# Cross attention of a decoder layer: the sums of the exponentials of groups 0 and 2 go from TensorE to VectorE, and four smaller steps change place

## The chip, the cores and the metric

One core of one Trainium2 chip runs the whole kernel. The metric is the device time of one execution in microseconds (us); lower is better. Engines are named as the profile names them: PE is TensorE (matmuls; PEld its weight loads), DVE is VectorE, ACT is ScalarE, POOL is GpSimd, SP issues most DMAs.

## The reference

Four batch entries of 512 rows and 512 columns, float32, 16 heads of 32 columns. The output is x after three steps:

```python
x = x + attn(layernorm(x), q_w, q_b, k_w, k_b, v_w, v_b, o_w, o_b)  # causal, masked to -inf
x = x + xattn(layernorm(x), ctx, ctx)   # heads of layernorm(x) as queries, of ctx as keys and values
x = x + ffn(layernorm(x), W_up, W_down, W_gate, W_expert)

# xattn, per head:
scores = einsum('bhqd,bhkd->bhqk', qh, kh) / sqrt(hd)
scores = where(causal, scores, -10000.0)          # a finite bias: masked keys keep a weight
out    = einsum('bhqk,bhkd->bhqd', softmax(scores), vh)
# ffn: relu(x Wup) Wdown + (sum of the softmax of the two largest gate logits) * (x Wexpert)
```

Because the masked bias of cross attention is finite, the kernel adds what the masked keys weigh: the weight of one masked key (`count`, from the row's maximum) times the sum of the values behind the diagonal (`beh_t`), and times their number (`cnt`) in the denominator.

## The kernel before

Everything is kept in float32 (the maxima's rows in bf16). The order on PE, DVE, ACT and POOL is the order in which the program issues its instructions (`tc.manual_schedule`); each engine works through its own queue, and a buffer of a pool is handed out again once its last reader is done. PSUM is four buffers of two banks (`pair`): scores, values' products, projections and transposes all take turns in them. In SBUF, `act` has one buffer per tag, `work` two unless `bufs` says otherwise.

The main loop runs over the batch entries b = 0 to 3. For each:

- `with_maxima` (L826) for self attention: ten units of score matmuls (L286), whose row maxima are needed for the softmax. ACT copies the scores (L297), POOL masks the diagonal (L305), DVE takes maxima (L317) and splits them into bf16 parts (`split`, L334 to L343). Between the units PE does filler: projections of the same or the next entry and the feed-forward part (`ffn`) of the entry before. `rows(g)` (L345) lets PE transpose the parts of one group of four heads into a row (L349), which DVE or ACT copies out (L355).
- `attend` (L869): ten units u0 to u9 of scores with the maximum subtracted (`scores`, L383 and L394), exponentials on ACT (L414), masks on POOL (L422). Two units later `values` (L434, matmuls on L453) multiplies them with v. In the units, (g, j) is head group g and block j of 128 keys: (0,0); (0,3),(0,1); (0,2),(1,2); (1,0); (1,3),(1,1); then the same for groups 2 and 3.
- the denominators. In `shares`, u = 0 is the product with v and u = 1 the product with `ones`, that is the sum of the exponentials. For groups in `self.added` the sums are made on DVE instead: `add_up` (L478) adds each block's exponentials into the block-0 tile (`self.sums`), and one set of four matmuls (`summed`, L487) reduces it over the keys. In self attention that holds for groups 0 to 2, in cross attention for none. `inverse` (L506) transposes, inverts and transposes back on DVE; `scale` (L502) multiplies on POOL; `divide` (L518) does the whole of it for the other groups, in cross attention with the masked keys' part added (L523, L524) before, and the product (L528) on DVE.
- `out_projection` (L657): the product with wo (`pm_o`, L663), transposes of ctx as filler, then the layer norm for the queries of cross attention (L675, L194 to L206).
- the same again for cross attention, and `add_cross` (L686): PE transposes the result (`tp_x`, L691), DVE adds it to x and takes the layer norm for `ffn`.

What only cross attention has: `behind(e, c)` (L643), a running sum from the right of the context's columns on DVE (L648), issued in `attend` before each group's first block; and `masked(g)` (L359): one matmul that spreads the row's maximum (L362), one exponential on ACT (L364), and two multiplications on DVE (L367 for the values, L368 for the count), issued in `attend` after units 2, 4, 7 and 9.

The feed-forward part of entry b runs as filler later: for b = 1 its expert matmuls lie in the maxima stage of self attention of b = 3 (`expert`, weighed into x by DVE on L790), for b = 2 its up and down projections lie in the maxima stage of cross attention of b = 3 (`down`, added to x by DVE on L775).

Of the kernel before, what the change touches and what calls it, by code (L numbers as in the profile page):

```python
# [9 lines left out]
F32 = mybir.dt.float32  # L10
# [16 lines left out]
def decoder_layer(  # L27
# [234 lines left out]
    class Attention:  # L262
        def __init__(self, q_t, k_t, v, cross, name):
            self.q_t, self.k_t, self.v, self.cross, self.name = q_t, k_t, v, cross, name
            self.nm, self.mrow, self.pv, self.out = {}, {}, {}, None
            self.more, self.sums, self.rden, self.e = {}, {}, {}, None
            self.added = () if cross else range(NC - 1)

        def maxima(self, pieces):

# [87 lines left out]

        def masked(self, g):  # L359

            bc = pair(f"mb_{self.name}_{g}")
            nc.tensor.matmul(bc[:, 0, :], lhsT=same, rhs=self.mrow[g], start=True, stop=True)  # L362
            count = work.tile([P, S], F32, tag="count", name=f"ct_{self.name}_{g}")
            nc.scalar.activation(count, bc[:, 0, :], AF.Exp, bias=mbias)  # L364

            beh = self.e.beh_t[:, g, :]
            nc.vector.scalar_tensor_tensor(beh, count, 1.0, beh, ALU.min, ALU.mult)  # L367
            nc.vector.scalar_tensor_tensor(count, count, 1.0, cnt, ALU.min, ALU.mult)  # L368
            self.more[g] = (beh, count)

        def scores(self, pieces):


            at, N = [], 0
            for g, j in pieces:
                at.append(N)
                N += S - j * P
            name = f"{self.name}_{pieces[0][0]}_{pieces[0][1]}"
            scs = [pair(f"sc_{name}_{n}") for n in range(2)]
            for (g, j), c in zip(pieces, at):  # L380
                for r in range(HG):
                    h = slice(r * HD, (r + 1) * HD)
                    nc.tensor.matmul(  # L383
                        scs[r // 2][:, r % 2, c : c + S - j * P],
                        lhsT=self.k_t[h, g, j * P : (j + 1) * P],
                        rhs=self.q_t[h, g, j * P :],
                        start=(c == 0),
                        stop=False,
                        skip_group_check=(len(pieces) > 1),
                    )  # L390
            for (g, j), c in zip(pieces, at):
                for r in range(HG):
                    h = slice(r * HD, (r + 1) * HD)
                    nc.tensor.matmul(  # L394
                        scs[r // 2][:, r % 2, c : c + S - j * P],
                        lhsT=onesb[h, :],
                        rhs=self.mrow[g][h, j * P :],
                        start=False,
                        stop=True,
                        skip_group_check=(len(pieces) > 1),  # L400
                    )
            g, j = pieces[0]
            pts = []
            if j == 0 and g in self.added:

                self.sums[g] = act.tile(
                    [P, 2, 2, S], F32, tag=("ck_t", "beh_t")[g % 2], name=f"sum_{name}"
                )
            for n in range(2):
                if j == 0 and g in self.added:  # L410
                    pt = self.sums[g][:, n]
                else:
                    pt = work.tile([P, 2, S], F32, tag="pt", name=f"pt_{name}_{n}", bufs=6)
                nc.scalar.activation(pt, scs[n], AF.Exp)  # L414

                if len(pieces) == 1:
                    diagonal = pt[:, :, :P].unsqueeze(2)
                elif j == pieces[1][1]:
                    diagonal = pt.rearrange("p u (k q) -> p u k q", k=2)[:, :, :, :P]
                else:  # L420
                    diagonal = pt[:, :, : 2 * P].rearrange("p u (k q) -> p u k q", k=2)
                nc.gpsimd.affine_select(  # L422
                    out=diagonal,
                    in_=diagonal,
                    compare_op=ALU.is_ge,
                    fill=0.0,
                    base=0,
                    pattern=[[0, 2], [0, len(pieces)], [1, P]],
                    channel_multiplier=-1,
                )  # L430
                pts.append(pt)
            return [(g, j, c, pts) for (g, j), c in zip(pieces, at)]
# [8 lines left out]
        def shares(self, g, blocks):  # L441

            js = {j for j, *_ in blocks}
            first = js == {0} if g % 2 == 0 else js == {2}
            last = js == {2} if g % 2 == 0 else 1 in js
            if first:
                self.pv[g] = pair(f"pv_{self.name}_{g}")
            pv = self.pv[g]
            for u in range(1 if g in self.added else 2):
                for n, (j, c, pts) in enumerate(blocks):  # L450
                    for r in range(HG):
                        h = g * HG + r
                        nc.tensor.matmul(  # L453
                            pv[r * HD : (r + 1) * HD, u, j * P :],
                            lhsT=ones if u else self.v[:, j, h * HD : (h + 1) * HD],
                            rhs=pts[r // 2][:, r % 2, c : c + S - j * P],
                            start=first,
                            stop=last and n == len(blocks) - 1,
                            skip_group_check=True,
                        )  # L460
            if first and g == 0 and not self.cross:
                self.out = act.tile([P, NC, S], F32, tag="o_t", name=f"oT_{self.name}")
            if (first if g in self.added else js == {0}) and g - 1 in self.added:
                self.sum_in = pv if g in self.added else pair(f"ls_{self.name}")
                self.summed(g - 1, self.sum_in)
            if js == {0} and g - 2 in self.added:
                self.scale(g - 2)
            if 1 in js and g - 1 in self.added and g not in self.added:
                self.spread(g - 1, self.sum_in)
                self.scale(g - 1)  # L470
            if last and g in self.added:
                nc.scalar.copy(self.out[:, g, :], pv[:, 0, :])
                if g > 0:
                    self.spread(g - 1, pv)
            elif last:
                self.divide(g)

        def add_up(self, made):  # L478
            for g, j, c, pts in made:
# [21 lines left out]

        def scale(self, g):  # L502
            o = self.out[:, g, :]
            nc.gpsimd.tensor_tensor(o, o, self.rden.pop(g), ALU.mult)

        def inverse(self, g, den):  # L506
            name = f"{self.name}_{g}"
# [8 lines left out]
            return den_t  # L516

        def divide(self, g):  # L518
            pv = self.pv.pop(g)
            num, den = pv[:, 0, :], pv[:, 1, :]  # L520
            if self.cross:
                beh, count = self.more.pop(g)
                nc.vector.tensor_tensor(count, den, count, ALU.add)  # L523
                nc.vector.tensor_tensor(beh, num, beh, ALU.add)  # L524
                num, den = beh, count
                self.out = self.e.beh_t
            rden = self.inverse(g, den)
            nc.vector.tensor_tensor(self.out[:, g, :], num, rden, ALU.mult)  # L528


    class Entry:
# [125 lines left out]
    def out_projection(e, a, sides):  # L657
# [3 lines left out]
        for c in range(NC):  # L661
# [7 lines left out]
                )  # L669
            if c < NC - 1:  # L670
                run(sides[c::3])

        def add(t):
            xi = e.x[:, t, :]
# [38 lines left out]
    def ffn(e):  # L713
# [55 lines left out]
        def down(t):  # L769
            if t % 2 == 0:  # L770
                made["d"] = pair(f"pm_d{b}_{t}")
            yield from project(made["d"][:, t % 2, :], made["h"], wdown_sb, t)
            if t % 2 == 1:
                both = e.x[:, t - 1 : t + 1, :]
                nc.vector.tensor_tensor(both, made["d"], both, ALU.add)  # L775

        def expert(t):
# [5 lines left out]
                made["e"] = pair(f"pm_e{b}_{t}")  # L783
            yield from project(made["e"][:, t % 2, :], f_t, wexp_sb, t)
            for n in (0,) if last else (0, 1) if t % 2 == 1 else ():
                weigh(t - t % 2 + n, made["e"][:, n, :], slice(0, D), nc.sync)

        def weigh(t, ps, cols, queue):
            xt = e.x[:, t, cols]
# [36 lines left out]
    def with_maxima(steps, a, first=0, norms=()):  # L826
# [16 lines left out]
        for n, pieces in enumerate(units):  # L843
# [6 lines left out]
            for k in range(count):  # L850
                next(fill, None)
                done += 1
                if k == min(1, count - 1) and n in (5, 7):
                    jobs = a.rows((n - 5) // 2) + jobs
                if n == len(units) - 1 and k == count - (2 if count > 4 else 1):
                    if total >= 2 * len(units):
                        a.rows(2)[0](nc.scalar.copy)
# [11 lines left out]
    def attend(a, late):  # L869
# [3 lines left out]
        for g in range(0, NC, 2):  # L873
            units += [[(g, 0)], [(g, 3), (g, 1)], [(g, 2), (g + 1, 2)]]
            units += [[(g + 1, 0)], [(g + 1, 3), (g + 1, 1)]]
        waiting, held = [], []

        def values():
            made = waiting.pop(0)
# [9 lines left out]
        for n, pieces in enumerate(units):  # L889
# [3 lines left out]
                    copy(nc.scalar.copy)  # L893
            if len(waiting) > 2:
                values()
            if a.cross and pieces[0][1] == 0:
                behind(a.e, pieces[0][0])
            if a.cross and n % 5 in (2, 4):
                a.masked(pieces[0][0])
        while waiting:  # L900
            values()

    with tc.manual_schedule(engines=BY_HAND):
# [11 lines left out]
        for b in range(B):  # L915
# [15 lines left out]
            run(steps[2:3])  # L931
            norm_cross(e, made, 2)
            ca = Attention(e.cq_t, e.ck_t, e.cv, True, f"c{b}")
            ca.e = e
            late = with_maxima(steps[3:], ca)
            if b + 2 < B:
                after.x = load_x(b + 1)
# [77 lines left out]
```

## Time and profile before

| | |
|---|---|
| median of 3 runs | 817.24 us (816.1 to 817.62) |
| the profiled execution | 814.9 us, span of its instructions 813.2 us |
| granted TensorE clock | 1.0 |
| PE busy | 802.2 us (99%) |
| DVE busy | 538.4 us (66%) |
| ACT busy | 395.6 us (49%) |
| POOL busy | 288.7 us (36%) |
| `pv_c` with `ones` (L453) | 512 matmuls, 43.2 us |
| `pv_c` with cv (L453) | 512 matmuls, 44.1 us |
| scans `behT` (L648) | 16, 20.5 us on DVE |
| additions `sum_s` (L483) | 72, 59.8 us on DVE |

The busy time of PE counts matmuls that overlap in the pipeline, so what a matmul costs is better read from the starts of the one and of the next in the timeline. A line of a timeline has the start, the time from the first to the last instruction of a run of equal ones, engine, source line, operation, result and operands, sizes, how many, and in brackets how long the engine was idle before and what ended that. Times are in us from the start of the span.

### The profile page before, as it was taken

How to read it: one execution, taken by the hardware profiler on the slowest of the kernel's cores; microseconds unless marked ns; L12 is line 12 of the kernel's file. 1: busy time of each engine (PE TensorE's matmuls, PEld its weight loads, DVE VectorE, ACT ScalarE, POOL GpSimd, SP SyncE). 2: the span in 40 equal slices, each digit the busy share in tenths (PEclk: the TensorE clock that was granted, in tenths of full speed). 3: DMA queues.
4: the chain of work that ended last, by engine and by line, in shares of the span. 5: the costliest groups of instructions: out<-in, count | busy, mean ns of one | idle time of the engine just before them, and what ended most of it. 6: DMA issues, size and time to landing. Idle time of an engine off the chain costs nothing.

```text
span 813.2 us, 14284 instructions
## 1 busy us (share of the span) xinstructions
PE 802.2 (99%) x5808; PEld 383.4 (47%) x5808; DVE 538.4 (66%) x930; ACT 395.6 (49%) x446; POOL 288.7 (36%) x485
## 2 busy tenths in 40 slices
PE   8999999999999999999999999999998999999998
PEld 7444554444444454444544445444444444444544
DVE  2478835868678834586867773687779844997512
ACT  2457426861546514566145752686166714574110
POOL 4334612342234732234233481244233643333100
PEclk9999999999999999999999999999999999999999
DMA  9600000001010000030100000000100100000101
GB/s 337 232 27 28 1 1 1 1 2 53 1 27 27 2 1 1 0 106 2 52 14 14 1 2 0 1 1 2 53 26 27 53 1 0 1 2 2 52 0 52
DMA packets 13681, 24.52 MB, mean 30 GB/s; under 512 B 1968, under 2 KB 2224, under 8 KB 13616
## 3 DMA queue, kind: packets, MB, share of 16 engines
q1 hardware_dynamic: 13184, 22.96, 8.3%
q8 instruction: 45, 0.74, 0.4%
q10 hardware_dynamic: 432, 0.66, 0.2%
q14 instruction: 20, 0.16, 0.1%
HBM read 19.42 MB, written 4.19 MB: 29 GB/s over the span
## 4 chain that ended last, share of the span: by engine, by line
PE 90%; DVE 8%; ACT 2%; DMA 0%; issue 0%; ACTq 0%
PE pm_qk L235 13%; PE pv_c L453 9%; PE pm_u L235 7%; PE pm_o L663 7%; PE pm_v L223 6%; PE pm_e L223 6%; PE sc_c L383 5%; PE pv_s L453 5%; PE pm_d L223 5%; PE sm_s L286 5%; PE sm_c L286 5%; PE sc_s L383 4%; DVE nm_s L317 3%; DVE nm_c L317 2%; PE sc_s L394 1%; ACT sum_s L414 1%
## 5 line engine op out<-in xcount | busy, mean ns | idle before, releaser
L317 DVE TENSOR_REDUCE nm_c<-s_c 128x2 f32<-128x1024 f32 (+3 forms) x128 | 96.1, 811 | 37.4 <-POOL s_c L305 37.4
L317 DVE TENSOR_REDUCE nm_s<-s_s 128x2 f32<-128x1024 f32 (+3 forms) x128 | 96.9, 811 | 35.2 <-POOL s_s L305 35.2
L297 ACT COPY s_s<-sm_s 128x1024 f32<-128x1024 f32 x80 | 77.1, 1015 | 64.4 <-PE sm_s L286 34.9
L297 ACT COPY s_c<-sm_c 128x1024 f32<-128x1024 f32 x80 | 77.1, 1015 | 44.4 <-PE sm_c L286 23.5
L414 ACT ACTIVATE pt_c<-sc_c 128x1024 f32<-128x1024 f32 x80 | 76.8, 1029 | 30.4 <-PE sc_c L394 30.4
L305 POOL TENSOR_SCALAR_AFFINE_SELECT s_c<-s_c 128x512 f32<-128x512 f32 (+1 forms) x80 | 44.1, 552 | 115.0 <-ACT s_c L297 115.0
L422 POOL TENSOR_SCALAR_AFFINE_SELECT pt_c<-pt_c 128x512 f32<-128x512 f32 (+1 forms) x80 | 54.9, 693 | 71.5 <-ACT pt_c L414 71.0
L305 POOL TENSOR_SCALAR_AFFINE_SELECT s_s<-s_s 128x512 f32<-128x512 f32 (+1 forms) x80 | 43.9, 551 | 90.8 <-ACT s_s L297 90.8
L483 DVE TENSOR_TENSOR sum_s<-sum_s,pt_s 128x256 f32<-128x256 f32 (+2 forms) x72 | 59.8, 895 | 15.0 <-PE pv_s L453 14.9
L414 ACT ACTIVATE pt_s<-sc_s 128x1024 f32<-128x1024 f32 x56 | 54.0, 1028 | 14.4 <-PE sc_s L394 8.8
L223 PE MATMUL pm_d<-wdown_sb,hT 128*128 128x512 f32 x128 | 60.9, 608 | 0.0
L235 PE MATMUL pm_u<-fT,wup_sb 128*128 128x512 f32 x128 | 59.1, 604 | 0.0
L223 PE MATMUL pm_v<-wv_sb,xnT 128*128 128x512 f32 x128 | 58.8, 600 | 0.0
L663 PE MATMUL pm_o<-wo_sb,oT_s 128*128 128x512 f32 x128 | 57.8, 596 | 0.0
L383 PE MATMUL sc_s<-qT,kT 32*128 32x128 f32 (+3 forms) x512 | 54.3, 462 | 3.4 <-DVE x L790 2.3
L235 PE MATMUL pm_qk<-xnT,wk_sb 128*128 128x512 f32 x120 | 57.3, 607 | 0.0
L223 PE MATMUL pm_e<-wexp_sb,fT 128*128 128x512 f32 x120 | 56.8, 606 | 0.0
L235 PE MATMUL pm_qk<-xnT,wq_sb 128*128 128x512 f32 x120 | 56.7, 604 | 0.0
L422 POOL TENSOR_SCALAR_AFFINE_SELECT pt_s<-pt_s 128x512 f32<-128x512 f32 (+1 forms) x56 | 47.6, 859 | 20.4 <-ACT pt_s L414 19.8
L383 PE MATMUL sc_c<-cqT,ckT 32*128 32x384 f32 (+3 forms) x512 | 51.5, 462 | 1.0 <-ACT pt_c L414 0.6
L286 PE MATMUL sm_s<-kT,qT 32*128 32x512 f32 (+3 forms) x512 | 47.5, 461 | 0.1
L286 PE MATMUL sm_c<-ckT,cqT 32*128 32x512 f32 (+3 forms) x512 | 46.1, 460 | 0.0
(150 smaller groups left out, 1195.9 us busy)
## 6 DMA issues: line engine op xcount, KB each, us to landing
cv<-in_ctx_dram SPq DMA_DIRECT2D x16, 256.0 KB, 4.3
out_dram<-x SPq DMA_DIRECT2D x15, 256.0 KB, 2.0
x<-in_x_dram SPq DMA_DIRECT2D x14, 256.0 KB, 4.1
xin<-in_x_dram SPq DMA_DIRECT2D x12, 256.0 KB, 2.7
wq_sb<-in_wq_dram SPq DMA_DIRECT2D x2, 512.0 KB, 6.1
wk_sb<-in_wk_dram SPq DMA_DIRECT2D x2, 512.0 KB, 7.8
wv_sb<-in_wv_dram SPq DMA_DIRECT2D x1, 1024.0 KB, 8.3
wo_sb<-in_wo_dram SPq DMA_DIRECT2D x1, 1024.0 KB, 9.9
```

What stands on the lines that cost most here:

```text
L223: nc.tensor.matmul(pm, lhsT=lhs_t[:, c, t * P : (t + 1) * P], rhs=w[:, c, :], start=(c == 0), stop=(c == NC - 1),)
L235: nc.tensor.matmul(pm, lhsT=w[:, c, f * P : (f + 1) * P], rhs=rhs_t[:, c, :], start=(c == 0), stop=(c == NC - 1),)
L286: nc.tensor.matmul(scs[r // 2][:, r % 2, c : c + (i + 1) * P], lhsT=self.q_t[h, g, i * P : (i + 1) * P], rhs=self.k_t[h, g, : (i + 1) * P] ...
L297: nc.scalar.copy(s, scs[n])
L305: nc.gpsimd.affine_select(out=diagonal, in_=diagonal, compare_op=ALU.is_ge, fill=NEG, base=0, pattern=[[0, 2], [0, len(pieces)], [-1, P]], ...
L317: nc.vector.tensor_reduce(self.nm[g][:, i, 2 * n : 2 * n + 2], made[n][:, :, c : c + (i + 1) * P], axis=AX.X, op=ALU.max, negate=True,)
L383: nc.tensor.matmul(scs[r // 2][:, r % 2, c : c + S - j * P], lhsT=self.k_t[h, g, j * P : (j + 1) * P], rhs=self.q_t[h, g, j * P :], start= ...
L414: nc.scalar.activation(pt, scs[n], AF.Exp)
L422: nc.gpsimd.affine_select(out=diagonal, in_=diagonal, compare_op=ALU.is_ge, fill=0.0, base=0, pattern=[[0, 2], [0, len(pieces)], [1, P]], ...
L453: nc.tensor.matmul(pv[r * HD : (r + 1) * HD, u, j * P :], lhsT=ones if u else self.v[:, j, h * HD : (h + 1) * HD], rhs=pts[r // 2][:, r % ...
L483: nc.vector.tensor_tensor(to, to, pts[n][:, :, c : c + S - j * P], ALU.add)
L663: nc.tensor.matmul(pms[t // 2][:, t % 2, :], lhsT=a.out[:, c, t * P : (t + 1) * P], rhs=wo_sb[:, c, :], start=(c == 0), stop=(c == NC - 1),)
```

## The change

1. In cross attention, groups 0 and 2 are in `self.added`: their exponentials are summed on DVE, and the four matmuls of `summed` write into the second bank of the group's own pv buffer. The sums' tiles share the buffer of self attention's v.
2. The four scans of `behind` are issued in `out_projection`, after the context's second transpose, and no longer in `attend`.
3. `masked(0)` and `masked(1)` are issued in the maxima stage (units 6 and 8), `masked(2)` and `masked(3)` after units 3 and 5 of `attend`; the multiplications of the latter two follow one unit later, behind the divisions of groups 0 and 1. The `count` tiles use the four buffers of tag `xn`.
4. The product with the inverse goes to POOL for groups 0 to 2 of cross attention; group 3 stays on DVE.
5. `aside`: the last expert block of entry 1 and the last down block of entry 2 are copied out of PSUM by ACT (with the weight as scale) and added to x by POOL, in place of DVE.

```diff
-            self.added = () if cross else range(NC - 1)
+            self.added = (0, 2) if cross else range(NC - 1)
...
-            count = work.tile([P, S], F32, tag="count", name=f"ct_{self.name}_{g}")
+            count = work.tile([P, S], F32, tag="xn", name=f"ct_{self.name}_{g}", bufs=4)
             nc.scalar.activation(count, bc[:, 0, :], AF.Exp, bias=mbias)
 
             beh = self.e.beh_t[:, g, :]
-            nc.vector.scalar_tensor_tensor(beh, count, 1.0, beh, ALU.min, ALU.mult)
-            nc.vector.scalar_tensor_tensor(count, count, 1.0, cnt, ALU.min, ALU.mult)
             self.more[g] = (beh, count)
+
+            def weigh(of, by):
+                nc.vector.scalar_tensor_tensor(of, count, 1.0, by, ALU.min, ALU.mult)
+
+            return [lambda: weigh(beh, beh), lambda: weigh(count, cnt)]
...
                 self.sums[g] = act.tile(
-                    [P, 2, 2, S], F32, tag=("ck_t", "beh_t")[g % 2], name=f"sum_{name}"
+                    [P, 2, 2, S],
+                    F32,
+                    tag="v" if self.cross else ("ck_t", "beh_t")[g % 2],
+                    name=f"sum_{name}",
                 )
...
-            if first and g == 0 and not self.cross:
+            if self.cross:
+                if first and g - 1 in self.added:
+                    self.summed(g - 1, self.pv[g - 1])
+                    self.divide(g - 1)
+                if js == {0} and g > 0:
+                    self.scale(g - 1)
+                if last and g not in self.added:
+                    self.divide(g)
+                    if g == NC - 1:
+                        self.scale(g)
+                return
+            if first and g == 0:
                 self.out = act.tile([P, NC, S], F32, tag="o_t", name=f"oT_{self.name}")
...
             o = self.out[:, g, :]
-            nc.gpsimd.tensor_tensor(o, o, self.rden.pop(g), ALU.mult)
+            engine = nc.vector if self.cross and g == NC - 1 else nc.gpsimd
+            engine.tensor_tensor(o, o, self.rden.pop(g), ALU.mult)
...
         def divide(self, g):
             pv = self.pv.pop(g)
-            num, den = pv[:, 0, :], pv[:, 1, :]
-            if self.cross:
-                beh, count = self.more.pop(g)
-                nc.vector.tensor_tensor(count, den, count, ALU.add)
-                nc.vector.tensor_tensor(beh, num, beh, ALU.add)
-                num, den = beh, count
-                self.out = self.e.beh_t
-            rden = self.inverse(g, den)
-            nc.vector.tensor_tensor(self.out[:, g, :], num, rden, ALU.mult)
+            beh, count = self.more.pop(g)
+            nc.vector.tensor_tensor(count, pv[:, 1, :], count, ALU.add)
+            nc.vector.tensor_tensor(beh, pv[:, 0, :], beh, ALU.add)
+            self.rden[g] = self.inverse(g, count)
...
             if c < NC - 1:
                 run(sides[c::3])
+            if c == 1:
+                for g in range(NC):
+                    behind(e, g)
...
-            if t % 2 == 1:
+            if t == NT - 1 and b == B - 2:
+                for n in range(2):
+                    aside(f"d{b}_{n}", t - 1 + n, made["d"][:, n, :], 1.0)
+            elif t % 2 == 1:
                 both = e.x[:, t - 1 : t + 1, :]
                 nc.vector.tensor_tensor(both, made["d"], both, ALU.add)
...
-                weigh(t - t % 2 + n, made["e"][:, n, :], slice(0, D), nc.sync)
+                u = t - t % 2 + n
+                if t == NT - 1 and b == B - 3:
+                    aside(f"e{b}_{n}", u, made["e"][:, n, :], made["rw"][:, u : u + 1])
+                    nc.sync.dma_start(out=out[b, u * P : (u + 1) * P, :], in_=e.x[:, u, :])
+                else:
+                    weigh(u, made["e"][:, n, :], slice(0, D), nc.sync)
+
+        def aside(name, t, ps, scale):
+            some = work.tile([P, D], F32, tag="xn", name=f"some_{name}", bufs=4)
+            nc.scalar.mul(some, ps, scale)
+            xt = e.x[:, t, :]
+            nc.gpsimd.tensor_tensor(xt, xt, some, ALU.add)
...
                     jobs = a.rows((n - 5) // 2) + jobs
+                if k == min(1, count - 1) and a.cross and n in (6, 8):
+                    jobs += a.masked((n - 6) // 2)
...
             if len(waiting) > 2:
                 values()
-            if a.cross and pieces[0][1] == 0:
-                behind(a.e, pieces[0][0])
-            if a.cross and n % 5 in (2, 4):
-                a.masked(pieces[0][0])
+            run(todo)
+            todo = a.masked(n // 2 + 1) if a.cross and n in (3, 5) else []
...
-            ca.e = e
+            ca.e, ca.out = e, e.beh_t
```

More of the change, by code (lines that the diff above doesn't have):

```diff
@@ L475, in shares @@
             elif last:
-                self.divide(g)
+                num, den = pv[:, 0, :], pv[:, 1, :]
+                nc.vector.tensor_tensor(
+                    self.out[:, g, :], num, self.inverse(g, den), ALU.mult
+                )
         def add_up(self, made):
@@ L875, in attend @@
             units += [[(g + 1, 0)], [(g + 1, 3), (g + 1, 1)]]
-        waiting, held = [], []
+        waiting, held, todo = [], [], []
         def values():
```

## The prediction, made before the change was run

> **What bounds the kernel now.** I read the page first: engines (part 1), the chain that ended last (part 4). Then the timeline of TensorE and of VectorE through one cross attention, and the groups by form.
>
> ```profile
> span 813.2 us, 14284 instructions
> PE 802.2 (99%) x5808; PEld 383.4 (47%) x5808; DVE 538.4 (66%) x930; ACT 395.6 (49%) x446; POOL 288.7 (36%) x485
> PE 90%; DVE 8%; ACT 2%; DMA 0%; issue 0%; ACTq 0%
> ```
> TensorE (PE) is busy all the time and is 90% of the chain, so a matmul taken out shortens the kernel unless PE then waits. The 8% of VectorE (DVE) are places where it is already last. The timeline of PE in batch 0 (start, duration):
>
> ```profile
> 156.35 0.39 PE L349 MATMUL mt_c<-identb,parts 128*128 128x128 bf16 x4
> ...
> 162.35 1.04 PE L453 MATMUL pv_c<-pt_c,ones 128*32 128x512 f32 x8
> 163.32 0.39 PE L362 MATMUL mb_c<-mrow_c,same 128*128 128x512 bf16 x1
> ...
> 165.12 0.40 PE L349 MATMUL mt_c<-identb,parts 128*128 128x128 bf16 x4
> 165.44 1.07 PE L453 MATMUL pv_c<-pt_c,cv 128*32 128x128 f32 x16
> 166.33 1.05 PE L453 MATMUL pv_c<-pt_c,ones 128*32 128x128 f32 x16
> ...
> 194.70 1.91 PE L691 MATMUL tp_x<-ident,behT 128*128 128x128 f32 x16
> ```
> The "ones" matmuls are what the change removes for groups 0 and 2. The two L349 groups transpose the mask rows of groups 2 and 3, and need DVE's `split`. DVE there:
>
> ```profile
> 155.76 0.23 DVE L343 TENSOR_TENSOR parts<-rest_c,parts 128x16 bf16<-128x16 f32 x1
> 155.86 4.71 DVE L317 TENSOR_REDUCE nm_c<-s_c 128x2 f32<-128x768 f32 x6
> ...
> 161.84 0.23 DVE L343 TENSOR_TENSOR parts<-rest_c,parts 128x16 bf16<-128x16 f32 x1
> ```
> Split 2 ends at 155.99, 0.36 before PE uses it; split 3 at 162.07, 3.05 before. From 144.37 to 162.07 DVE has no gap, so work put into that stretch moves both splits. Last, the price of an addition:
>
> ```profile
> 73.24 4.57 DVE L483 TENSOR_TENSOR sum_s<-sum_s,pt_s 128x256 f32<-128x256 f32 x6
> 87.64 5.71 DVE L483 TENSOR_TENSOR sum_s<-sum_s,pt_s 128x256 f32<-128x256 f32 x6
> 87.81 1.44 POOL L504 TENSOR_TENSOR oT_s<-oT_s,dt_s 128x512 f32<-128x512 f32 x1
> ```
> Six additions make one group's sum: 4.57 us in one case, 5.71 beside GpSimd's (POOL's) `scale`, with the same shapes. Undisturbed, the forms start 0.33, 0.86 and 0.57 apart (256, 768 and 512 wide), two of each: 3.5.
>
> **PE's saving.** Per group the ones go: 0.89 (v to ones is 165.44 to 166.33) for block 0, 0.89 for blocks 3 and 1, 0.43 for block 2 (169.06 to 169.49), together 2.2. `summed` comes in: four heads, 0.86 (the ls_s group stands 93.92 to 94.78). Net 1.35 a group, 2.7 a batch, 10.8 over four.
>
> **What DVE pays.** In the listing of the changed order, units u0 to u9 of `attend` are (0,0), (0,3)+(0,1), (0,2)+(1,2), (1,0), (1,3)+(1,1), then the same for groups 2 and 3. I follow batch 0; all times are this profile's.
>
> *Maxima stage.* Mask weights of groups 0 and 1 come here: two matmuls (mb to u8: 180.62 to 180.94, 0.32 each) delay PE by 0.64. Two multiplications each (starts 181.84, 182.57, next at 183.18) cost DVE 1.33 per group. One pair stands before split 2, both before split 3. Split 2 then ends at 157.32 and PE is there at 156.99: it waits 0.39 with hand-over (0.06, from batch 3's L343 to L349). u0 starts at 157.69 instead of 156.66. Split 3 ends at 164.73; PE, rid of u0's ones and of mb, is there at 164.5: 0.3 lost.
>
> *First sum.* The six additions start at 164.65 and end by 169.2 at 4.57. PE does pv u1 (0.89), mb 2 (0.32), u4 (about 1.3, held 0.4 by a PSUM buffer that ScalarE (ACT) frees), pv of u2 (1.3), and is at `summed(0)` at 169.3: no wait. u5 starts at 170.2, before 170.79.
>
> *Second sum.* DVE runs divide(0) (five operations, 169.75 to 172.72: 2.97) and the weights of group 2, is idle from 174.7, and must wait for pv u4 for divide(1). PE from 170.2: u5 1.30, pv u3 1.86, mb 0.32, u6 1.30, pv u4 1.86, so 176.84. Hand-over 0.2: divide(1) 177.0 to 180.0, weights of group 3 to 181.3. Only then come group 2's six additions. Bounds 3.5 and 5.7; I take 4.9, since POOL's scale(1) (1.33, released at 180.0, behind the selects of u7 that last to 180.8) overlaps the first two and selects the others: 186.25. PE from 176.84: u7 1.3, v of u5 0.97, u8 1.3, v of u6 0.97, u9 1.3, three pv pieces of u7 1.3, so at `summed(2)` at 184.0. It waits 2.3 (0.95 to 3.1 by the bounds). Behind it in PE's queue stand pv u8 and u9 (3.56), the filler (3.54) and tp_x; DVE's divide(3) waits for those. tp_x starts at 186.25+0.86+3.56+3.54 = 194.2, before 194.70: **0.5 gained in batch 0**, not 2.7. Batch 2 has the same rows 384.7 later: 0.5.
>
> [...]
>
> *Batch 1.* More filler: DVE was idle 2.92 before 345.56, which swallows the first pair, and split 2 (352.83) is far ahead of PE (355.69). Only 0.64 is lost before u0 and nothing at split 3: 36.2 from u0 to tp_x against 37.9, gain 1.05.
>
> *Batch 3.* DVE has no gap before split 2 (714.25), and PE already waits 0.31 for it. It moves 1.33: u0 at 715.95 for 714.64. `aside` takes the 1.13 of L775 out (715.31 to 716.44), so split 3 is at 724.0 and PE is there at 722.7: 1.3 lost, 1.0 more than in batch 0. The first sum costs 0.3, and u4 is not held this time (0.4). From u0 to tp_x 36.5+1.0+0.3-0.4 = 37.4: tp_x at 753.35 for 752.56, loss 0.8.
>
> *`aside` in self attention of batch 3.*
>
> ```profile
> 623.18 1.40 DVE L790 SCALAR_TENSOR_TENSOR x<-pm_e,rw,x 128x512 f32<-128x512 f32 x2
> 624.63 1.14 PE L383 MATMUL sc_s<-qT,kT 32*128 32x128 f32 x12 [2.30 <-DVE x L790]
> ```
> PE waits 2.30 for a PSUM buffer that DVE empties behind its maxima. Two ACT copies (0.59 each, as L472) directly after ACT's copies (end 620.92) free it at 622.1. Next late is split 2 (622.44), before PE wants it (623.6). DVE is rid of 1.3 too, so split 3 keeps ahead. Gain 2.2; the two POOL additions (1.27 each) end at 624.2, ahead of the selects that pv u0 needs at 626.
>
> **Covered, costing nothing.** The four scans (1.22, starting 1.14 apart) lie in the 13.2 us in which DVE waits for pm_o: from 292.95 they end at 297.6, the add starts at 298.01. In batch 3 they end 0.5 late; xn_q, at 673.12 before, is then ready at 673.6, just as tp_q wants it (673.63). Without that cover 4.6 a batch. scale(0) and (1) end 12 us before tp_x, scale(2) at 191.6; scale(3) on DVE ends 194.5, wanted at 195.5. `sum_c` in v's buffer: the old v is read out, the new one is written after tp_x. The memsets (0.1 each) go where POOL waits for mv_q, 9.3 us even in batch 3.
>
> **Sum.** 0.5+1.05+0.5-0.8+2.2 = 3.45. The profiled execution took 814.9 (span 813.2 and 1.7 around it), so 811.45 by its own time; it lies 2.3 under the median of 817.24, which I take as the scale: **813.8**. A difference under 0.2% (1.6 us) can't be told from none.
>
> **Rivals.**
> A. [...] Additions cost 3.5; the wait at `summed(2)` falls to 0.95, 1.35 more per batch: 817.24-3.45-5.4 = 808.4. For: POOL is only 36% busy. Against: both rows above have POOL's selects or scale beside them. The full saving, 10.8+2.2, needs additions done by 184.0, 2.7 us after they can begin: under the lowest bound. 804 I nearly exclude.
> B. *Slower: DVE's additions take 5.7 at both sums,* as beside L504. The second ends 0.8 later in four batches. The first ends at 170.35, 1.05 after PE, in batches 0, 2 and 3 (in 1 DVE is ahead). 3.2+3.15 = 6.35: 817.24-3.45+6.35 = 820.1. It decides from 0.9 a batch on, where the 3.45 are eaten. For: scale(0) and scale(1) both fall beside DVE's two-input work. Against: no scale is near the first sum, and DVE idles 2.2 before divide(1), which takes up a late start.
> C. *`aside` does not pay:* the two copies push ACT's first exponentials, the wait at u1 becomes one at u2. The 2.2 go: gain 1.25, 816.0, no difference.
>
> **Numbers.** My forecast 0.48 (811 to 816.5), A 0.17, B 0.20, C 0.15. The range goes from A to near B: 808 to 819.5. Faster: 0.41 of mine, A, 0.03 of C: 0.61. Slower: B and 0.02: 0.22. Same: 0.17.
>
> **What would show it.** In the new profile: `ones` groups on pv_c halved to 256, and 64 new matmuls on sum_c; a wait of PE of about 2.3 us for DVE `sum_c` before the second `summed` in each batch, little before the first; waits of 0.3 to 1 for `parts` before the L349 groups of g=2 and 3, most in batch 3; no wait before u1 in batch 3's self attention; sum_c additions of 4.6 to 5 us a group. Wrong it is if the second wait is missing (A), if it is over 3 us or the first over 0.6 (B), or if the 2.30 turns up at u2 (C).

## The result, and the profile after

The changed kernel takes 820.31 us (median of 5 runs, 820.23 to 820.75), the kernel before 817.58 on the same chip (816.10 to 817.88). The ratio is 1.0042, with a 95% interval of 1.0029 to 1.0056: 0.4% slower, where 813.8 was forecast. The executions of the kernel before differ among themselves by up to 3 us, and most of those beside the experiments, 33 of 51, have a mean granted clock of 0.996 to 0.998 (last section). The profiled one (814.9) has 1.0, and so have all five of the changed kernel; like with like, the change costs 820.31 - 814.9 = **5.4 us**.

The page of the changed kernel, engines and chain, to be laid beside those of before:

```profile
span 818.6 us, 13942 instructions
PE 796.5 (97%) x5616; PEld 378.9 (46%) x5616; DVE 569.6 (70%) x963; ACT 398.1 (49%) x450; POOL 310.7 (38%) x501
PE 80%; DVE 16%; issue 1%; ACT 1%; DMA 0%; DVEq 0%
```
TensorE's busy time did fall, by 5.7 us, but VectorE's share of the chain doubled from 8% to 16%. Where TensorE idles, by what it waits for (total, times, longest):

```profile
PE pv_c L512 <- DVE sum_c L506: 6.8, 4, 1.7
PE mt_c L349 <- DVE parts L343: 4.2, 6, 1.0
PE mt_s L349 <- DVE parts L343: 2.6, 2, 1.5
```
These are the second sum, the splits of the cross maxima, and the splits of the last self attention. The table has the length of stages on TensorE, from the first matmul of one kind to that of the next, in the profiled executions (e1 to e11 are the experiments below):

| stage, us | before | after | e1 | e3 | e4 | e8 | e9 | e11 |
|---|---|---|---|---|---|---|---|---|
| cross maxima, batch 0 (sm_c to sc_c) | 30.56 | 32.12 | 32.12 | 32.13 | 32.12 | 32.12 | 32.12 | 30.99 |
| cross maxima, batch 1 | 44.40 | 44.84 | 44.84 | 44.84 | 44.84 | 44.84 | 44.84 | 44.84 |
| cross attention, batch 0 (sc_c to tp_x) | 38.03 | 38.33 | 36.43 | 36.69 | 37.26 | 36.14 | 35.40 | 35.53 |
| cross attention, batch 1 | 37.89 | 38.33 | 36.43 | 36.69 | 37.26 | 36.15 | 35.40 | 35.40 |
| self attention, batch 3 (sc_s to pm_o) | 32.65 | 31.96 | 31.96 | 31.97 | 31.97 | 31.96 | 31.96 | 31.37 |
| cross maxima and attention, batch 3 | 73.65 | 75.34 | 73.45 | 73.71 | 74.27 | 73.16 | 72.42 | 71.34 |

Batch 2 repeats batch 0. From before to after: 2 x (1.56 + 0.30) + (0.44 + 0.44) + 1.69 - 0.69, less 0.19 by which the first stages were shorter, makes 5.4, the whole difference of the spans. All other stages are equal to 0.01. The forecast had 0.5 + 1.05 + 0.5 - 0.8 + 2.2 gained in the same places: the cross maxima and attention of every batch came out worse than forecast, by 2.4, 1.9, 2.4 and 0.9 us, and the last self attention by 1.5.

Batch 0 on TensorE, VectorE, GpSimd and ScalarE (start, duration), against the groups shown of before:

```profile
157.70 0.40 PE L349 MATMUL mt_c<-identb,parts 128*128 128x128 bf16 x4 [0.96 <-DVE parts L343]
...
165.86 0.40 PE L349 MATMUL mt_c<-identb,parts 128*128 128x128 bf16 x4 [0.36 <-DVE parts L343]
...
171.39 1.14 PE L387 MATMUL sc_c<-cqT,ckT 32*128 32x512 f32 x8
...
187.36 1.66 PE L512 MATMUL pv_c<-sum_c,ones 128*32 128x512 f32 x6 [1.70 <-DVE sum_c L506]
...
192.82 3.70 PE L223 MATMUL pm_v<-wv_sb,xnT 128*128 128x512 f32 x8
196.36 1.91 PE L714 MATMUL tp_x<-ident,behT 128*128 128x128 f32 x16
```
```profile
187.36 0.14 PEld L512 LDWEIGHTS pv_c<-sum_c,ones 128*32 128x32 f32 x4 [2.18 <-DVE sum_c L506]
188.40 0.11 PEld L512 LDWEIGHTS pv_c<-sum_c,ones 128*32 128x32 f32 x2 [0.90 <-DVE sum_c L506]
```
```profile
149.58 0.92 DVE L371 SCALAR_TENSOR_TENSOR behT<-ct_c,behT 128x512 f32<-128x512 f32 x1
150.53 0.88 DVE L371 SCALAR_TENSOR_TENSOR ct_c<-ct_c,cnt 128x512 f32<-128x512 f32 x1
...
165.68 4.13 DVE L506 TENSOR_TENSOR sum_c<-sum_c,pt_c 128x256 f32<-128x256 f32 x6
...
182.70 5.64 DVE L506 TENSOR_TENSOR sum_c<-sum_c,pt_c 128x256 f32<-128x256 f32 x6
```
```profile
182.21 1.70 POOL L528 TENSOR_TENSOR behT<-behT,dt_c 128x512 f32<-128x512 f32 x1
183.86 1.16 POOL L429 TENSOR_SCALAR_AFFINE_SELECT pt_c<-pt_c 128x256 f32<-128x256 f32 x2
```
```profile
185.95 1.94 ACT L421 ACTIVATE pt_c<-sc_c 128x1024 f32<-128x1024 f32 x2 [2.21 <-DVE sum_c L506]
```
TensorE waits at both L349 groups and at the second L512 group, as foreseen, and not at the first. Its weight loads (PEld) wait for the second sum twice: 2.18 us for the first half of it, and 0.90 more for the second half. The second set of additions begins 1.4 us later than forecast (182.70 for 181.3) and takes 5.64 in place of 4.9. `scale(1)` on GpSimd stands beside its first additions and ahead of the selects of u8. Not foreseen: ScalarE's exponentials of u9 also wait 2.21 us for VectorE, which still has to read the `pt` buffers that they would overwrite.

### The profile page after: what moved, and what is told of

Read it like the earlier page. It is cut to its first block, busy times and chain, and to the rows that moved or that the text cites. A ratio compares the mean times of both kernels' runs of the same rounds, so it can differ in the third digit from the quotient of the medians.

```text
span 818.6 us, 13942 instructions
## 1 busy us (share of the span) xinstructions
PE 796.5 (97%) x5616; PEld 378.9 (46%) x5616; DVE 569.6 (70%) x963; ACT 398.1 (49%) x450; POOL 310.7 (38%) x501
## 4 chain that ended last, share of the span: by engine, by line
PE 80%; DVE 16%; issue 1%; ACT 1%; DMA 0%; DVEq 0%
PE pm_qk L235 11%; PE pm_u L235 7%; PE pm_o L683 7%; PE pm_v L223 6%; PE pm_e L223 6%; DVE nm_c L317 5%; PE pv_s L460 5%; PE pm_d L223 5%; PE pv_c L460 5%; PE sm_s L286 5%; PE sc_s L387 4%; PE sm_c L286 3%; PE sc_c L387 3%; DVE nm_s L317 3%; DVE sum_c L506 2%
## 5 line engine op out<-in xcount | busy, mean ns | idle before, releaser
L421 ACT ACTIVATE pt_c<-sc_c 128x1024 f32<-128x1024 f32 x64 | 61.7, 1029 | 22.1 <-PE sc_c L398 11.0
L429 POOL TENSOR_SCALAR_AFFINE_SELECT pt_c<-pt_c 128x512 f32<-128x512 f32 (+1 forms) x64 | 45.7, 717 | 35.1 <-ACT pt_c L421 35.1
L387 PE MATMUL sc_s<-qT,kT 32*128 32x384 f32 (+3 forms) x512 | 53.0, 462 | 0.9 <-ACT sum_s L421 0.6
L257 ACT COPY fT<-tp_f 128x1024 f32<-128x1024 f32 x8 | 8.0, 1013 | 80.8 <-PE tp_f L251 80.8
```

The lines of the kernel that those rows point to most:

```text
L387: nc.tensor.matmul(scs[r // 2][:, r % 2, c : c + S - j * P], lhsT=self.k_t[h, g, j * P : (j + 1) * P], rhs=self.q_t[h, g, j * P :], start= ...
L429: nc.gpsimd.affine_select(out=diagonal, in_=diagonal, compare_op=ALU.is_ge, fill=0.0, base=0, pattern=[[0, 2], [0, len(pieces)], [1, P]], ...
```

## Experiments

Theories. **D**: VectorE reaches the end of the second sum too late, because other work stands ahead of the additions and GpSimd's stretch them. Rivals: **P**, TensorE's saving is given back to ScalarE and the PSUM buffers whatever VectorE does; **S**, the exponentials and selects of u7 hold the additions; and smaller ones named in each expectation.

**e1, the first sum alone.**

```diff
-            self.added = (0, 2) if cross else range(NC - 1)
+            self.added = (0,) if cross else range(NC - 1)
```


> The changed kernel with the sum of cross group 0 alone (group 2's denominators as matmuls with ones, as before). Theory D (VectorE is late at the second sum): the 1.70 us wait at the denominators of group 2 goes in each batch and 1.35 us of TensorE work comes back, so about 1.4 us faster than the changed kernel's 820.3: 818.9. Rival P (the time that TensorE saves is given back anyway, because ScalarE's exponentials and the PSUM buffers set the pace): the second sum cost its wait and saved nothing, so 4 x 1.70 less: 813.5.

Measured: 812.88 (812.79 to 813.02), ratio to before 0.9963 (0.9949 to 0.9977). The second sum cost 7.4 us, as P had it, not the 1.4 of D: more than its four waits of 1.70. Batch 1 from sm_c to tp_x went from 82.29 before to 81.27, so the first sum is worth 1.0 a batch where TensorE does not wait for VectorE.

**e2, the second sum alone** (`(2,)` in the same line).

> The changed kernel with the sum of cross group 2 alone. Theory D: the first sum was worth its 1.35 us of TensorE work a batch, or at the least the 0.2 us by which u5 still came early once the 1.16 us of late u5 are taken off: 821 to 825.7. Rival P: the first sum brought nothing: 820.3.

Measured: 822.66, so the first sum is worth 2.35 us within the changed kernel: inside D's range, at its low end. P's 820.3 is out, so TensorE's saving is not all given back.

**e3, weights of group 3 behind the additions.**

```diff
-            run(todo)
-            todo = a.masked(n // 2 + 1) if a.cross and n in (3, 5) else []
+            if n not in (6, 7):
+                run(todo)
+                todo = []
+            if a.cross and n in (3, 5):
+                todo = a.masked(n // 2 + 1)
```


> The changed kernel with the two masked-weight products of cross group 3 issued on VectorE behind the six additions of group 2, in place of ahead of them. Theory D: the additions start 1.7 us earlier (181.0 for 182.7 in batch 0) and the 1.70 us wait at the denominators of group 2 goes in each batch: 813.5. [...]

Measured: 813.88, 6.4 us faster than the changed kernel by the order of two instructions in each batch. The additions start at 181.26 and the wait is 0.27:

```profile
181.26 5.68 DVE L506 TENSOR_TENSOR sum_c<-sum_c,pt_c 128x256 f32<-128x256 f32 x6
186.87 1.12 DVE L371 SCALAR_TENSOR_TENSOR behT<-ct_c,behT 128x512 f32<-128x512 f32 x1
```
D holds. S allows 814 at best (the author's estimate, from selects that end at 185.0 in the changed kernel), which 813.88 alone would hardly exclude, but its mechanism is not in the trace: they are the selects of u8 (183.86, 256 wide), those of u7 end at 182.2, and VectorE has no idle time before or between the additions, there or here. But with its wait nearly gone the second sum still gains nothing over e1 (36.69 for 36.43 of attention), so D is not the whole.

**e4, no products on GpSimd.**

```diff
         def scale(self, g):
+            if self.cross and g < NC - 1:
+                self.rden.pop(g)
+                return
```


> The changed kernel without GpSimd's products of cross groups 0 to 2 by their reciprocals (these three products are left out, the output lacks them). Theory L (VectorE's two-input instructions and GpSimd's hold each other up, as the 256-wide addition of 1.49 us beside the 1.70 us product): the additions of the second sum fall from 5.64 us to about 4.8 and the second weight product from 1.00 to 0.7, so 1.1 us of the 1.70 us wait goes in each batch: 816. Rival N (the lengths come from VectorE itself): the same 5.64 us, 820.3.

Measured: 816.16, 4.15 off, as L had it. The additions start where they did, and are 1.07 shorter:

```profile
182.69 4.57 DVE L506 TENSOR_TENSOR sum_c<-sum_c,pt_c 128x256 f32<-128x256 f32 x6
```
So three products on an engine that was 38% busy cost 1.04 us a batch, through the additions beside them.

**e5, weights of groups 0 and 1 behind the first sum.**

```diff
...
-                    jobs += a.masked((n - 6) // 2)
+                    a.late_weighs.append(a.masked((n - 6) // 2))
...
+            if n in (3, 4) and a.late_weighs:
+                run(a.late_weighs.pop(0))
             run(todo)
```


> The changed kernel with the four masked-weight products of cross groups 0 and 1 issued on VectorE in the attention itself: those of group 0 behind the six additions of group 0, those of group 1 behind the division of group 0. Their matmuls and exponentials stay in the maxima stage. Theory D (the products hold up the splits): TensorE's waits of 0.96 and 0.36 us ahead of the rows of groups 2 and 3 go in batches 0 and 2, those of 0.76 and 0.82 in batch 3 only in part: 2.6 to 4.2 us off 820.3, so 817. Rival P (what is saved there is given back at the PSUM buffers of the scores): within 0.5 of 820.3.

Measured: 821.16 (820.36 to 823.28), no gain. The waits at the splits did go: maxima of 30.99 for 32.12 in batch 0, and 35.94 for 36.85 in batch 3. But the scores of u1 now take 1.61 us in place of 1.05, held by a buffer that ScalarE frees (its copy of the row ends at 158.55, u1 begins at 158.14), so part of each wait had only stood in for that; and the wait at the second sum grew from 1.70 to 1.98. In the profiled execution TensorE's clock fell behind that wait in batch 1, to a mean of 0.72 from 387 to 393, and by the lengths in batch 2 too: these two attentions took 40.14 and 40.05 us. That of batch 0, with the same wait and no drop in the lengths of its matmuls (1.66 for the first six behind the wait, 3.70 for `pm_v`, as in the changed kernel), took 38.75 (38.33 in the changed kernel). So the two drops cost 2.7 us by these lengths, and without them the edit would have gained 1.8 (an estimate from these lengths and the spans, 819.5 and 818.6). e10 tests it without that wait.

**e6, without the two places of `aside`**, and **e7, with its GpSimd additions later.** In e6 both conditions are made false, so that VectorE adds from PSUM as before. In e7:

```diff
...
-            nc.gpsimd.tensor_tensor(xt, xt, some, ALU.add)
+            later.append(lambda: nc.gpsimd.tensor_tensor(xt, xt, some, ALU.add))
...
         for n, pieces in enumerate(units):
+            if n == 1:
+                for add in later:
+                    add()
+                later.clear()
```


> The changed kernel without the two places where ScalarE copies a PSUM buffer aside and GpSimd adds it: VectorE does these additions from PSUM as before. [...] Rival, the prediction's step: 2.2 - 0.8 = 1.4 us slower, 821.7.

> The changed kernel with the four GpSimd additions of the set-aside tiles (and the stores behind them) issued behind the second unit of scores, in place of at once; ScalarE's copies stay where they are. Theory L (the additions hold up the small VectorE steps of the splits: 1.20 and 1.21 us where 0.18 and 0.20 are usual): the waits of 1.10 and 1.53 in the last self attention go and those of 0.76 and 0.82 in the last cross attention shrink: 2.6 to 4 us off, 817. Rival M (VectorE's maxima are late there for reasons of their own): 820.3.

Measured: e6 825.22 (823.68 to 826.86), 4.9 slower, and beyond the 821.7 of the prediction's step; e7 820.55, no change. In e6 the 2.30 us wait is back at u1 of the last self attention and another of 1.71 appears in the last cross attention, and behind the first the clock is 0.50 from 629 to 632 and 0.55 from 632 to 636, and the stage takes 35.12 us; the same stage, with the same wait and a clock of 1.00, takes 32.65 in the kernel before. So 2.5 of the 4.4 us by which e6's profiled span is longer (823.0 for 818.6) are the price of the clock. In e7 the last self attention is 31.37 (0.6 better, a part of what L says) and the last cross attention 0.5 worse (39.00 of attention for 38.49; the wait at its second split is 1.32 for 0.82): the two cancel, so only the additions of the expert tiles should be late. What they do where they stand, in the changed kernel (first TensorE, then VectorE, then GpSimd):

```profile
629.04 0.40 PE L349 MATMUL mt_s<-identb,parts 128*128 128x128 bf16 x4 [1.10 <-DVE parts L343]
634.76 0.40 PE L349 MATMUL mt_s<-identb,parts 128*128 128x128 bf16 x4 [1.53 <-DVE parts L343]
```
```profile
626.15 1.20 DVE L341 TENSOR_TENSOR rest_s<-nm_s,parts 128x16 f32<-128x16 f32 x1
627.38 1.21 DVE L342 CAST parts<-rest_s 128x16 bf16<-128x16 f32 x1
```
```profile
626.04 2.49 POOL L825 TENSOR_TENSOR x<-x,some_e 128x512 f32<-128x512 f32 x2 [0.24 <-ACT some_e L823]
```
Two steps of `split` on 16 columns, the second a cast with one input, take 1.2 us each, as long as one GpSimd addition (2.49 for two); undisturbed they take 0.18 and 0.20 (before, 621.76 and 621.98). With the additions moved away (e7) they are as quick again:

```profile
625.92 0.19 DVE L341 TENSOR_TENSOR rest_s<-nm_s,parts 128x16 f32<-128x16 f32 x1
626.15 0.20 DVE L342 CAST parts<-rest_s 128x16 bf16<-128x16 f32 x1
```

**e8, e3 with the second denominators one unit later.**

```diff
-                if first and g - 1 in self.added:
+                if (first if g == 1 else g == 3 and js == {0}) and g - 1 in self.added:
```


> The kernel of e3 with the denominators of group 2 and its division issued one unit later still, behind the values of the full unit of group 3. Theory D: the 0.27 us wait goes, and the four column groups of the array no longer fall out of step where two wait for one half of the sum and two for the other (the stretch from those matmuls to the projection is 5.24 us in e3 where 4.4 us of work lie), so about 1.1 us a batch off e3's 813.9: 809.5. Rival E (the division of group 2, now later, meets that of group 3 on VectorE and holds up the transposes behind the attention): 1 us a batch lost again: 813 to 816.

Measured: 812.31, 1.6 off e3 where D had 4.4. The wait is gone, but the stretch that should come into step does not: the weight loads for the values of u8 now wait for GpSimd, and from there the matmuls go in pairs instead of fours:

```profile
185.32 0.21 PEld L460 LDWEIGHTS pv_c<-pt_c,cv 128*32 128x32 f32 x4 [0.20 <-POOL pt_c L429]
186.15 0.11 PEld L460 LDWEIGHTS pv_c<-pt_c,cv 128*32 128x32 f32 x2 [0.61 <-POOL pt_c L429]
```
GpSimd does `scale(1)` first (182.21, 1.96 us) and the selects behind it.

**e9, e8 with `scale(1)` behind the last selects.**

```diff
-                if js == {0} and g > 0:
-                    self.scale(g - 1)
+                if js == {0} and g in (1, 3):
+                    if g == 3:
+                        self.scale(1)
+                    self.scale(g - 1)
```


> The kernel of e8 with GpSimd's product of group 1 issued behind the selects of the last two units of exponentials, in place of ahead of them. Theory G (GpSimd's queue is the cover that fails): the 1.96 us product stands ahead of the two selects that the values of the full unit of group 3 need, and TensorE's weight loads wait 0.61 us for them; it also stretches the 256-wide additions beside it. About 0.6 us a batch off e8's 812.3: 809.9. Rival X (ScalarE's exponentials come too late for the selects to matter): 812.3 within 0.4.

Measured: 809.26, 3.05 off e8. The loads of u8 no longer wait for GpSimd, the matmuls from there to the projection stay in step (4.41 us, 185.43 to 189.84, for 5.15 in e8), and the additions fall from 5.68 to 4.61:

```profile
185.21 0.35 PEld L460 LDWEIGHTS pv_c<-pt_c,cv 128*32 128x32 f32 x8
```
**e10, e9 with the edit of e5; e11, e10 with the expert additions of `aside` as in e7.**

> The kernel of e9 with, in addition, the edit of e5 (the four masked-weight products of groups 0 and 1 behind the first sum). In e5 the maxima stages became 1.13, 0, 1.13 and 0.91 us shorter and the attention of batch 0 0.42 longer, and TensorE's waits of 1.98 us at the second sum were followed by a lower granted clock; here there is no such wait. Theory D: 3.2 less 4 x 0.2 to 0.4, so 1.6 to 2.4 us off e9: 808 if e9 is 809.9. Rival P (the scores' PSUM buffers take it all back): e9's time within 0.4.

> The kernel of e10 with, in addition, the two GpSimd additions of the set-aside expert tiles (and their stores) issued behind the second unit of scores. In e7 that made the last self attention 0.6 us shorter: 0.6 off e10. Rival M: no change within 0.2.

Measured: 806.52, 2.7 off e9 (a little over the 1.6 to 2.4 of D; P is out), and 806.05, 0.5 off e10. e11 keeps every part of the change, in another order, and beats both kernels: ratio to before 0.9878 (0.9862 to 0.9893). Its chain, beside 80% and 16% above:

```profile
PE 87%; DVE 8%; ACT 3%; issue 1%; DMA 0%
```
**e12, the kernel before with `aside` alone.**

> The kernel before with the two set-aside places alone. Theory C (the 2.30 us wait of TensorE in the last self attention is in some executions followed by some 5 us at half the granted clock, which is why the kernel before has times from 814.7 to 818.0): without that wait all executions lie within 0.5 us of each other, and as the stage itself is 0.7 us shorter, 814.2 (less up to 0.5, or more by what the additions cost the last cross attention, 0.8): 813.7 to 815.0. Rival V (the spread has another source, the transfers at the start): the same spread of 3 us, median 0.7 us below that of the kernel before.

Measured: 814.19; 11 of 12 executions lie between 813.98 and 814.46, one at 816.10. The kernel before, in the 17 executions beside it, went from 814.70 to 817.69. Without the 2.30 us wait the spread is gone, as C says, but for that one execution (mean clock 0.998), which stays unexplained.

## Why the prediction was wrong, point by point

- **Failed: the end of the second sum.** That VectorE would be late there, and TensorE wait, was right, and so was the path behind it: from the end of the additions to tp_x 8.02 us (7.95 forecast). The additions ended at 188.34, not 186.25. Of these 2.1 us, 0.7 are their length (5.64 for 4.9, nearly the upper bound of 5.7), and 1.4 their start, for u5 was already 1.2 late. TensorE itself came 1.7 late (185.66 for 184.0), so 2.3 + 2.1 - 1.7 = 2.7 us of waiting were due, of which its rows show 1.70. From the first denominators to the projection there are 5.46 us (187.36 to 192.82) with 4.4 us of work in them: 3.56 for the values of the last two units, as in the forecast, and 0.86 for the denominators. This 1.0 is no idle time in TensorE's rows, where the matmuls go in pairs; the weight loads show it, with 0.90 of waiting for the second half of the sum. 1.70 + 1.0 less 0.9 of saving make 1.8 a batch lost by the second sum; e1 has 1.90 (38.33 to 36.43).
- **Failed: "covered, costing nothing" for the GpSimd products.** That they ended early enough for tp_x was true and not the question. Leaving them out brought 4.15 us (e4), through the additions beside them, and one of them stood ahead of selects that TensorE needed (e8, e9). The 4.9 taken for the second additions was the author's estimate, between 3.5 and 5.7 and with a product of 1.33 beside them; the product took 1.70, the additions 5.64 beside it, and without any 4.57, not 3.5.
- **Failed: `aside`, 2.2 forecast, 0.69 measured** (32.65 to 31.96; 0.68 on the kernel before, e12). The wait at u1 went as forecast. The step that failed is that the POOL additions were followed only to the selects they might delay; the split of VectorE beside them, which they stretch by 2.0 us, was not looked at. e7 shows this cause, but brought back only 0.6 of the missing 1.5: there 0.48 us of waiting for ScalarE appears at u2, and the next split, beside the selects that queue behind the additions, takes 2.4 us for 0.9, which leaves a wait of 0.72.
- **Mis-sized: the splits in the maxima.** 0.39 and 0.3 forecast for batch 0, 0.96 and 0.36 measured. The first pair of weights took 1.75 from start to next start (149.58 to 151.33), not the 1.33 taken from before; both run into selects on GpSimd (149.53, 150.45). That 0.36 is close to 0.3 is luck: the second split ends 1.1 later than forecast (165.80 for 164.73), and TensorE comes 1.0 later too (165.50 for 164.5). In batch 3, 1.3 was forecast and the stage grew by 1.12. e10 shows what issuing these four products later is worth: 2.7 us.
- **Mis-sized: TensorE's saving.** 1.35 a group is the matmul time and right as such, but what reaches the end is 1.02 for the first sum (e1, batch 1) and 1.03 - 0.16 for the second once nothing holds it (e9 against e1; the division now ends later and returns 0.16 behind tp_x). The scores of u3 and u4 take 1.82 and 1.59 us in place of 1.3, held by PSUM buffers (their weight loads wait for ScalarE's exponentials, 0.84 and 0.17 us at u3, 0.23 at u4). Theory P is this part, a quarter to a third of the saving, and no more.
- **Failed: the scale to the median.** 2.3 us were added for the distance of the profile from the median. They belong to executions of the kernel before with a mean clock of 0.996 to 0.998; the change takes away the wait of 2.30 us behind which the clock fell in e6, and its median is its profiled time. The 2.3 went the right way by luck: by its own sum, 811.45, the forecast was 8.9 us off, not 6.5.
- **Right:** the matmuls that go and come; no wait at the first denominators; the wait at u1 gone; a wait before every L349 group named; the scans at no cost (pm_o to sm_c is 29.48 us in both kernels, and 25.49 in batch 3); no cost from the sums in v's buffer or from the memsets.
- **The rivals.** B gave 820.1, which is nearest, but by luck, as half its mechanism is missing: the second additions took 5.64, but the first took 4.13 and TensorE did not wait for them. What stands in its place are the later start, the loss in `aside` and the splits. A and C are out: the wait is there, and the 2.30 did not come back at u2 but, changed, at the next splits.

Of the 1.2 us by which u5 is late in batch 0, the early weights make 1.0: in e5, where they are behind the first sum and the matmuls of `pv_c` ahead of u5 take the 1.07 and 1.04 of the changed kernel, u5 starts at 170.43 in place of 171.39. What stays open is the rest of it, why moving the additions of the `down` tiles in e7 lengthens the wait at the next split, and the one longer execution of e12.

## What to carry to other kernels

Work moved to an idle engine isn't free because it ends in time: look at what runs beside it on the engine that it can hold up, and at what stands behind it in its own queue; here leaving out three products on GpSimd won back 4.15 us, where the change had cost 5.4. Where a new wait depends on a chain of one engine, put everything that is not needed yet behind that chain before judging the idea: the same sums gave 820.3 us with weights and products ahead of them, and 806.5 with these behind them and the second denominators one unit later (e10). When the executions of a kernel differ by more than the effect, compare the profiled stages, not the medians.

## What the runs showed of the hardware

**Behind a wait of 2.30 us TensorE's clock was 0.50 in e6** (TensorE, weight load, VectorE, ScalarE and GpSimd busy in each stretch, then the granted clock):

```profile
624.00:629.00 5.00, 2.82 (x20) 1.07 (x18) 4.86 (x10) 3.35 (x4) 1.62 (x4) 0.98 0.01 2
629.00:632.00 3.00, 2.88 (x24) 1.77 (x24) 3.00 (x6) 0.64 (x1) 0.07 (x1) 0.50 0.47 175
632.00:636.00 4.00, 4.00 (x34) 2.29 (x32) 2.18 (x5) 2.95 (x5) 1.35 (x3) 0.55 0.79 254
636.00:640.00 4.00, 3.73 (x48) 1.76 (x48) 3.62 (x5) 3.19 (x4) 2.71 (x4) 1.00 0.04 12
```
TensorE idles from 626.82 to 629.12 and then has about half its clock until about 635.5 (an estimate from the 0.50 and the 0.55). Not every execution shows it: of 51 executions of the kernel before beside the experiments, which has the same wait, 18 had a mean clock of 1.000 and took 814.7 to 815.1, and 33 had 0.996 to 0.998 and took 815.7 to 818.0. With four waits of 1.98 (e5) all 6 executions were at 0.994 to 0.998; with four of 1.70 (the changed kernel, e2 and e7) all 16 were at 0.999 or 1.000. One of the 12 executions of e12, in whose profile no wait of TensorE behind the first 10 us is over 1.53, was at 0.998 all the same. What decides which executions have the lower clock was not shown.

**VectorE instructions took longer beside GpSimd ones, small ones by as much as large ones**: 16 columns took 1.20 us beside a GpSimd addition of 1.2, six times the 0.18 to 0.20 of the kernel before and of e7, so 1.0 more; the first 256-wide addition of the second sum took 1.49 us beside the product of 1.70, for 0.41 in the kernel before (73.24, with no product beside it), so 1.1 more.

**The narrow matmuls of the values, which run four at a time, fell out of step in the changed kernel and in e8.** The matmuls of the values and the sums are 32 columns wide, one for each head of a group, and four run side by side: eight of them, 512 wide, take 0.85 us (e9, 185.43 to 186.28), where eight of 128 columns take 3.54 (192.82 to 196.36). Where the operand of two of them came later than that of the other two (their weight loads wait 0.90 us for VectorE in the changed kernel, 0.61 for GpSimd in e8), the profile shows them in pairs (x2 in place of x4 or x8) up to the projection, with no idle time in TensorE's rows. The stretch to the projection is 5.15 us (e8) to 5.46 (the changed kernel); in step it is 4.41 (e9).
